# Both jobs of a step between the two layers of the first attention, with three PSUM banks for jobs and two tiles for the first layer

## The chip, the cores and the metric

The kernel runs on one core of a Trainium2 chip. The metric is the device time of one execution in microseconds. The number to be explained is the median over repeated runs.

The core has a tensor engine (PE), a vector engine (DVE), a scalar engine (ACT), a general engine (POOL) and a DMA issuing engine (SP). Each takes its instructions in the order in which the program lists them. PE writes its products to PSUM[...]. A bank holds one tile of 128 x 512 floats. DVE or ACT must read a bank out before PE may write it again.

## The reference

The program is one decoder layer on `x` of 16 x 256 x 256: a first attention, a cross attention with a context, and a routed feed-forward of four experts. Each is followed by `x = layernorm(x + part(x))`. The change touches the first attention alone:

```python
Q, K, V = x @ wq + bq, x @ wk + bk, x @ wv + bv     # 16 heads of 16 values
def prep(t):                                         # the two layers
    h1 = tanh(einsum('bshd,do->bsho', t, w1) + b1)   # 16 -> 256
    return einsum('bsho,on->bshn', h1, w2) + b2      # 256 -> 16
qp, kp = prep(Q), prep(K)
# a fixed 8x8 mixing and a rotation among the first 8 batches, then
qq, kk = sum(qe ** 2, -1), sum(ke ** 2, -1)
s = qq[:, :, None, :] * kk[:, None, :, :]
out = einsum('bijh,bjhd->bihd', softmax(s / s, axis=2), V) @ wo + bo
```

## The kernel before

The 16 batches are taken in eight pairs (`q`, `NPAIR = 8`), with 512 tokens each. `TileContext` has the orders of PE, ACT and DVE set by hand (`manual_schedule`): each engine gets its instructions in the order in which the Python code issues them.

**The steps.** The first attention runs in steps `t` from 0 to 128 (`LAST`), 16 to a pair: 8 for keys (`side` 0) and 8 for queries (`side` 1). In each, `hidden(t)` makes half of the first layer's 256 outputs for four of the 16 heads: four products `ph<-qT,w1p` with a contraction of 32 rows, into two tiles of two banks each, and two tanh on ACT (L873, `h<-ph`, 128 x 1024). `outer(t - 1, ...)` makes the second layer of the step before: four products `pe<-h,w2p` of 32 columns each, gathered over four steps in one bank (pool `psAe`). After the fourth, DVE (`enc`, L890) or ACT (`sq`, L893) reads that bank out.

**The plan.** Everything else is listed in `Plan`. There are two kinds of entry:

- Entries with a fixed step (`plan.at`), which `plan.run(t)` issues: `scores` (DVE, L967, `z<-rqb,ra`), `exps` (ACT, L974, `z<-z`), `spread` (a DMA on SP's queue, `rqb<-rqd`) and `norm` (DVE and POOL).
- Jobs with a first and a last step (`plan.job`). `plan.take()` issues the one whose last step comes first. A job is a group of products or transposes on PE into one bank and the read-out of that bank by DVE (in a few cases ACT): `turn_x` (`ptx`), `project` (`pq`), `values` (`pv`), `rotate` (`pr`), `norms` (`p`), `queries` (`ptr`), `weigh` (`po`, the values weighed by `z`), `finish1` to `finish3` (`pn`, `pto`, `pf`). The generators that `fold` advances are jobs too: `pt`, `pp`, `pb` of the feed-forward's weights and `pex` of the cross attention's.

**A step's order**, in `step` (L1145 on): `hidden(t)`, one job, the fixed entries of `t`, `outer(t - 1)`, a second job. On PE this reads: `ph`, job, `pe`, job.

**PSUM** while the first attention runs:

```python
ps = heads.enter_context(tc.tile_pool(name="psA", bufs=1, space=PSUM))    # jobs
pse = heads.enter_context(tc.tile_pool(name="psAe", bufs=1, space=PSUM))  # second layer
psb = heads.enter_context(tc.tile_pool(name="psAb", bufs=3, space=PSUM))  # first layer, two banks each
```

This is 1 + 1 + 6 = 8 banks. All jobs share the single bank of `psA`. The first layer has three tiles and a step takes two, so the tiles of step `t + 1` are one that was free and the one that the first tanh of step `t` reads.

After step 128 these pools close. The cross attention's steps begin, and the last jobs of pair 7 are taken among them with the same `step` function.

## Time and profile before

| What | Value |
|---|---|
| Median of 3 runs | 1849.65 us (1845.53 to 1854.64) |
| The profiled execution, its own time | 1787.34 us |
| Its span, first to last instruction | 1785.6 us |
| Granted PE clock, mean over the span | 0.965 |
| PE / DVE / ACT / POOL busy over the span | 93% / 53% / 54% / 30% |
| First `ph` of step 0 | 11.87 us |
| First `ph` of step 9 | 45.22 us |
| First `ph` of step 127 | 560.09 us |
| `ph` products, `pe` products | 1024 records each (two for one product) |
| tanh (L873) | 256, 1112 ns each |

The profiled execution is 62 us shorter than the median of the runs. All durations here are of that execution.

A timeline row gives the start, the time until the last end, the engine, the line, the operation, the output and inputs by name, the shapes and the count. In brackets is the idle time of the engine before the row and what ended it. A step is read on PE from one `ph` row to the next. Ends of PE's products are modelled and lie about 0.1 us after the point where the next group may start, so the cost of a group is best read from start to start. A weight load (PEld) overlaps a product.

### The profile page before, as it was taken

Reading aid. Unit: us, or ns where it says so; the run is one execution under the profiler, and the core shown is the slowest. Engines: PE = TensorE matmul, PEld = TensorE weight load, DVE = VectorE, ACT = ScalarE, POOL = GpSimd, SP = SyncE. Lnnn points to the kernel's source line nnn. Section 1 sums busy time; section 2 is a strip of 40 time slices with the busy share of each in tenths; the row PEclk is TensorE's granted clock in tenths of the full one; section 3 lists DMA queues with packets and bytes.
Section 4 is the critical chain, followed back from the end, with each engine's and each line's share of the span. In section 5 each row is a group of like instructions: output and inputs, shape, how many; then the busy total and the mean of one; then the engine's idle time right before and its main releaser. Section 6 shows DMA issues by size and latency. Waiting matters only on the chain. (4 is left out here: it accounts for less than half of the span.)

```text
span 1785.6 us, 32366 instructions
## 1 busy us (share of the span) xinstructions
PE 1654.0 (93%) x12254; PEld 946.1 (53%) x12254; DVE 953.1 (53%) x2008; ACT 961.7 (54%) x1404; POOL 536.7 (30%) x1235
## 2 busy tenths in 40 slices
PE   7999999999999999999999999998999997899960
PEld 2343434343444566566565656655665666566640
DVE  2235556655555877877778676772113533122147
ACT  4556777776777766766666676654332112232242
POOL 5100313212123232445535464455321011121042
PEclk8999999999999999999999999998999999899985
DMA  9921211122212300001000000002241102321033
GB/s 262 295 81 61 68 61 61 62 70 78 65 61 72 107 14 2 15 3 38 26 15 29 11 26 9 32 26 80 75 147 50 48 13 66 109 66 42 29 98 112
DMA packets 117771, 115.34 MB, mean 65 GB/s; under 512 B 7776, under 2 KB 111408, under 8 KB 117584
## 3 DMA queue, kind: packets, MB, share of 16 engines
q1 hardware_dynamic: 108560, 93.08, 16.4%
q0 software_dynamic: 7824, 19.65, 3.7%
q8 instruction: 114, 1.87, 0.4%
q14 instruction: 73, 0.60, 0.1%
q10 hardware_dynamic: 1200, 0.15, 0.1%
HBM read 73.79 MB, written 38.54 MB: 63 GB/s over the span
## 5 line engine op out<-in xcount | busy, mean ns | idle before, releaser
L1329 DVE TENSOR_REDUCE mpad<-p 128x4 f32<-128x1024 f32 x256 | 310.6, 1216 | 107.2 <-PE p L119 104.7
L873 ACT ACTIVATE h<-ph,L_attn_b 128x1024 f32<-128x1024 f32 x256 | 271.3, 1112 | 158.5 <-PE ph L119 154.8
L1335 ACT ACTIVATE e<-p 128x512 f32<-128x512 f32 x512 | 276.4, 596 | 147.7 <-PE p L119 145.4
L119 PE MATMUL p<-qp,kT 32*128 32x256 f32 x2048 | 307.3, 402 | 1.4 <-ACT e L1335 0.6
L119 PE MATMUL p<-kT,qp 32*128 32x256 f32 x2048 | 292.6, 400 | 3.5 <-DVE mpad L1329 3.5
L119 PEld LDWEIGHTS p<-kT,qp 32*128 32x128 f32 x2048 | 183.4, 184 | 89.6 <-issue 45.2
L119 PEld LDWEIGHTS p<-qp,kT 32*128 32x128 f32 x2048 | 204.0, 185 | 7.1 <-issue 3.1
L119 PE MATMUL ph<-qT,w1p 32*128 32x512 f32 x1024 | 151.3, 648 | 3.0 <-ACT h L873 1.8
L967 DVE TENSOR_TENSOR z<-rqb,ra 128x1024 f32<-128x1024 f32 x120 | 151.5, 1265 | 3.8 <-DMA rqb<-rqd 3.5
L119 PE MATMUL pe<-h,w2p 128*32 128x512 f32 x1024 | 139.6, 617 | 1.9 <-ACT sq L893 1.0
L974 ACT ACTIVATE z<-z 128x1024 f32<-128x1024 f32 x120 | 127.1, 1060 | 1.3 <-DVE z L967 0.9
L119 PE MATMUL pob<-e,vaug 128*32 128x512 f32 x1024 | 125.9, 610 | 0.0
L632 POOL DMA_INDIRECT ya<-xlist,place x52 | 49.7, 956 | 199.9 <-DVE xs L642 68.9
L159 POOL TENSOR_SCALAR ln_ve<-ln_mv 128x2 f32<-128x2 f32 x32 | 7.2, 224 | 299.0 <-DVE ln_mv L157 298.8
L480 ACT ACT_TABLE_LOAD x18 | 23.1, 1283 | 114.1 <-PE pt L479 113.8
L119 PE MATMUL pw<-xeT,L_ffn_sw_w 128*128 128x512 f32 (+1 forms) x256 | 83.3, 486 | 1.3 <-ACT xeT L480 1.3
L163 POOL TENSOR_SCALAR xs<-xs,ln_mv,rs_y 128x256 f32<-128x256 f32 x64 | 83.2, 1305 | 3.5
L119 PE MATMUL po<-z,vaug 128*32 128x256 f32 x1024 | 72.8, 389 | 6.4 <-DVE ra L927 1.6
L119 PE MATMUL pr<-L_ffn_ml_w,hid 128*128 128x256 f32 x288 | 65.1, 388 | 8.5 <-ACT hid L547 8.5
L1384 POOL TENSOR_TENSOR ob<-o,o 128x256 f32<-128x256 f32 x32 | 23.2, 724 | 163.3 <-DVE o L1382 163.3
L119 PEld LDWEIGHTS ph<-qT,w1p 32*128 32x128 f32 x1024 | 42.7, 185 | 53.8 <-issue 42.0
L405 POOL DMA_INDIRECT xlist<-xs,place x64 | 62.8, 981 | 20.0 <-issue 17.3
(355 smaller groups left out, 2616.2 us busy)
## 6 DMA issues: line engine op xcount, KB each, us to landing
rqb<-rqd SPq DMA_DIRECT2D x64, 512.0 KB
xlist<-zero SPq DMA_DIRECT2D x16, 1024.0 KB
xe<-xlist SPq DMA_DIRECT2D x20, 512.0 KB
xlist<-ye SPq DMA_DIRECT2D x14, 512.0 KB
xs<-in_x SPq DMA_DIRECT2D x8, 512.0 KB
cx<-in_ctx SPq DMA_DIRECT2D x8, 512.0 KB
qp<-st SPq DMA_DIRECT2D x256, 2.0 KB
out<-xs SPq DMA_DIRECT2D x8, 512.0 KB
```

The costliest lines, as they stand in the source:

```text
L119: PE.matmul(out=out_, lhsT=lhsT, rhs=rhs, start=start, stop=stop)
L159: POOL.tensor_scalar(ve, mv[:, :, 1], EPS, None, ALU.add)
L163: POOL.tensor_scalar(x, x, mv[:, i, 0:1], r[:, i:i + 1], ALU.subtract, ALU.mult)
L405: put = POOL.indirect_dma_start(xlist[g][:], bass.IndirectOffsetOnAxis(ap=place[:, n, k:k + 1], axis=0), xs[:, q * CPB + n, :], None)
L480: copies[c](t[:, c, :n * P], pt[:, :n * P])
L632: POOL.indirect_dma_start(t[:, n, :], None, xlist[group(q)][:], bass.IndirectOffsetOnAxis(ap=moe["place"][:, q * CPB + n, k:k + 1], axis=0),)
L873: ACT.activation(h, phs[gp], AF.Tanh, bias=b1[:, fc:fc + 1])
L967: DVE.tensor_tensor(z, bc(rqbs[u][:, 2 * gp:2 * gp + 2], 2, 2), bc(rk, 3, S), ALU.mult)
L974: ACT.activation(z, z, AF.Exp)
L1329: DVE.tensor_reduce(mpads[j % 2][:, 2 * gp:2 * gp + 2, :, ic], p1, AX.X, ALU.max, negate=True)
L1335: ACT.activation(e[:, gi], p2[gi], AF.Exp)
L1384: POOL.tensor_tensor(o[:, ic], oas[0], oas[1], ALU.subtract)
```

## The change

`take` can now issue several jobs and keep those of one name (`behind`) to the end. `step` runs the fixed entries of `t` first, then takes both jobs, `weigh` behind the other, and only then issues `outer(t - 1)`. On PE a step reads `ph`, job, job, `pe`. The pools of PSUM become 3 banks for jobs, 1 for the second layer, and two tiles (4 banks) for the first layer: 8 again.

```diff
-    def take(self, slack=10**6):
+    def take(self, slack=10**6, n=1, behind=None):
 
-        if self.jobs:
-            best = min(self.jobs, key=lambda x: x[:2])
-            if best[0] <= self.now + slack:
+        held = []
+        for _ in range(n):
+            best = min(self.jobs, key=lambda x: x[:2], default=None)
+            if best is not None and best[0] <= self.now + slack:
                 self.jobs.remove(best)
-                best[2](*best[3])
+                if best[2].__name__ == behind:
+                    held.append(best)
+                else:
+                    best[2](*best[3])
+        for x in held:
+            x[2](*x[3])
...
-    ps = heads.enter_context(tc.tile_pool(name="psA", bufs=1, space=PSUM))
+    ps = heads.enter_context(tc.tile_pool(name="psA", bufs=3, space=PSUM))
     pse = heads.enter_context(tc.tile_pool(name="psAe", bufs=1, space=PSUM))
-    psb = heads.enter_context(tc.tile_pool(name="psAb", bufs=3, space=PSUM))
+    psb = heads.enter_context(tc.tile_pool(name="psAb", bufs=2, space=PSUM))
...
             if t < LAST:
                 hs = hidden(t)
-            plan.take()
             plan.run(t)
+            plan.take(n=2, behind="weigh")
             if last[0] is not None:
                 outer(t - 1, last[0])
             last[0] = hs
-            plan.take()
```

The cross attention's own plan calls `take` with its defaults, which do what they did.

## The prediction, made before the changed kernel was run

> **What bounds the kernel now.** I read the busy times by stage, then what PE waited for, then PE's timeline step by step. The stretch from step 9's first `ph` to step 127's holds the first attention at full load:

> ```profile
> core 0: us, PE busy (x) PEld busy (x) DVE busy (x) ACT busy (x) POOL busy (x), PEclk, DMA share, GB/s
> ...
> 45.22:560.09 514.87, 500.65 (x3652) 208.60 (x3648) 271.81 (x434) 357.42 (x362) 104.75 (x226) 0.99 0.28 87
> ```

> PE is busy 97%, ACT 69%, DVE 53%: PE sets the pace, 4.36 us a step (514.87 / 118). So only what shortens PE's own sequence or its waits can help. Those waits, in the same stretch:

> ```profile
> engine line waited for: us in total, times, longest us
> PE pex L1197 <- DVE scr L1195: 4.8, 3, 2.9
> PE po L119 <- DVE ra L927: 1.6, 2, 0.9
> PE ptx L838 <- PE ph L119: 1.5, 2, 0.7
> PE po L119 <- DVE xT L839: 1.4, 1, 1.4
> ...
> PE pb L119 <- PE pb L119: 0.5, 1, 0.5
> PE pb L119 <- DVE rowsof L269: 0.5, 1, 0.5
> ```

> With the rows left out the list sums to 14.1 us. `po` waiting for `ra` or `xT` is no matter of data: these read out the previous job's bank. The timeline shows one such step:

> ```profile
> 334.09 1.14 PE L119 MATMUL ph<-qT,w1p 32*128 32x512 f32 x8
> ...
> 335.16 1.98 PE L119 MATMUL pq<-xT,L_attn_wq 128*128 128x512 f32 x4
> 335.34 2.12 ACT L873 ACTIVATE h<-ph,L_attn_b 128x1024 f32<-128x1024 f32 x2 [2.48 <-PE ph L119]
> ...
> 337.07 1.07 PE L119 MATMUL pe<-h,w2p 128*32 128x512 f32 x8
> ...
> 338.07 0.66 PE L838 MATMUL ptx<-ident,xs 128*128 128x128 f32 x4
> ...
> 338.65 1.14 PE L119 MATMUL ph<-qT,w1p 32*128 32x512 f32 x8
> ...
> 340.45 0.66 DVE L839 COPY xT<-ptx 128x512 f32<-128x512 f32 x1
> ...
> 341.16 1.07 PE L119 MATMUL po<-z,vaug 128*32 128x256 f32 x16 [1.37 <-DVE xT L839]
> ```

> From start to start, `ph` takes 1.07, `pq` 1.91, `pe` 1.00, `ptx` 0.58. At 341.16 `po` has waited for DVE, which came late to `xT`. The ACT row gives the second figure I need: tanh begins 1.25 us after its `ph` and both take 2.12.

> [...] In the experts' stage groups of one mode follow without loss:

> ```profile
> 1329.13 1.04 PE L479 MATMUL pt<-ident,xe 128*128 128x128 f32 x8
> 1330.01 3.62 PE L119 MATMUL pw<-xeT,mw 128*128 128x256 f32 x16
> 1333.53 3.72 PE L119 MATMUL pr<-L_ffn_me_c2w,hid 128*128 128x256 f32 x16
> ```

> Eight transposes take 0.88, 0.11 each, so four are 0.43; between groups of other modes four took 0.58. `pq` takes 1.91 where its four records, 0.43 apart, make 1.71. A drain costs 0.15 to 0.20. [...] after the 2.9 us wait for `scr` at 415.6, PE ran at 0.50 from 417.2 to 420.6, and `pe` took 1.88. The 1.37 us wait above did not do it. [...] So with one bank, a job's products wait for the last read-out.

> **The change, part by part** (PE groups counted from both programs' instruction orders, steps 9 to 126).

> *Fewer drains.* A step's two jobs were each between two other modes. Now they adjoin, and in 48 steps both use the whole array. The order shows 404 changes of mode before and 357 after. 47 x 0.16 = **-7.5 us**. `weigh` behind the other job changes nothing here: `po` and `pe` share a mode (0.88 instead of 1.00) and adjoined before too.

> *Three banks for jobs.* Of the 14.1 us, 1.0 are the feed-forward's `pb`, a chain of data that stays. The rest waits behind a read-out or a late DVE. With three banks a group waits only for the job three before. To 13.1 I add 1.5 for the half clock after 415.6 (`po` 0.6, `pe` 0.9) and 1.5 for some fifteen waits that modelled ends shorten by 0.1: 16 us at stake. `pex` still needs `scr` of DVE in its own step; I take **-15** (-10 to -16).

> *Two tiles for the first layer.* Now `ph` of the next step waits for both tanh. The least distance of two `ph` is 1.25 + 2.12 + 0.11 (tanh end to product, from 30.50 to 30.61 below) = 3.48 us. With three tiles it was one tanh less:

> ```profile
> 29.44 2.12 ACT L873 ACTIVATE h<-ph,L_attn_b 128x1024 f32<-128x1024 f32 x2
> ...
> 30.61 1.24 PE L119 MATMUL ph<-qT,w1p 32*128 32x512 f32 x6 [1.77 <-ACT h L873]
> ...
> 42.00 2.12 ACT L873 ACTIVATE h<-ph,L_attn_b 128x1024 f32<-128x1024 f32 x2 [0.28 <-PE ph L119]
> ...
> 44.40 2.12 ACT L873 ACTIVATE h<-ph,L_attn_b 128x1024 f32<-128x1024 f32 x2 [0.28 <-PE ph L119]
> ```

> In the last two rows tanh pairs stand 2.40 apart. The new order has 28 steps shorter than 3.48: two without a job (2.07 long, 1.41 short each), seven with `po` alone (2.95, 0.53), seven with one or two small transposes (about 2.65, 0.83), twelve with two small groups (about 3.15, 0.33). 2.8 + 3.7 + 5.8 + 4.0 = **+16.3**. A longer step hides the wait, since `ph` starts later anyway; the average is 4.1. The lightest step keeps PE at work for half of 3.48 us; I expect no half clock.

> *Steps 0 to 8* have few jobs. Steps 6 to 8 took 2.07, 2.41 and 2.40; at 3.48 they cost +3.6. Steps 2 and 3 lose as much, but step 4 waits for ACT's sine tables (26.6 to 29.4) anyway. The first `pq` no longer waits for a bank, -1. Sum **+2.5** (0 to +5).

> *The end.* After step 127 jobs wait for the bank by 0.55, 0.55 and 0.89, and a half clock follows. That is 3.5 us; further on PE waits for `exps` of the last pair, so I take half, **-2**.

> *Moved at no cost.* The fixed entries now stand ahead of both jobs. On DVE, a score (1.22) precedes the first read-out; two banks more cover it, and with one bank it would cost PE up to 1.2 us a step. On ACT `exps` (1.05) precedes `rotate`'s square, needed a step later. On SP, `spread`'s DMA goes ahead of `queries`' store in the same step; no pair's spread needs a store of its own step. On POOL, `norm` goes ahead of `turn_x`'s add; POOL is busy 20%. `pe` moves behind both jobs: the tanh it reads ended a step before, and its bank is read out under the next `ph` (1.07) and jobs. DMAs keep their number and size. The later parts keep their order.

> **Sum**: -7.5 - 15 + 16.3 + 2.5 - 2 = -5.7, say -6 us. That is 1781 against the profiled 1787.3, and 1849.65 - 6 = **1843.5** against the median, which lies 62 us above the profiled execution. Its own range is -13 to +1. A measurement here can tell some 0.5%, 9.2 us, from no change, so the forecast lies inside that bound and its range crosses it.

> **The rivals.**

> *The tile wait is mostly hidden.* The runs take 3.5% longer than the profiled execution. If that is PE, steps lengthen, while tanh does not: at 4% the 16 us fall to about 14. If the early steps also cost nothing, all 16 us of waits go and the end keeps its 3.5, the change gives -7.7 - 16 + 14 - 3.5 = -13, and with drains at 0.20 -15: **1834.5**. For it: PE is the bound nearly everywhere. Against: the short steps are in the order, and the wait needs nothing unusual.

> *The tanh chain becomes the bound, slower.* Between two tanh pairs, ACT has 1.36 us for `exps` (1.05) and every fourth step a square (0.69). If a score comes late from DVE, which now reads out both jobs in a row, `exps` pushes the next tanh and the distance of two `ph` grows. At 3.7 the short steps sum to 27 us, at 3.9 to 38, at 4.0 to 44. The gains less the early loss are 22, so it decides from 3.6 on; 0.5% slower is reached at 3.8. At 3.9: -22 + 38 = +16, **1865.5**. For it: 56 of 118 steps lie under 3.7. Against: a score is issued a whole step before its `exps`, and DVE is half idle.

> *It does not do what it says*: the waits for banks turn into waits for the same late DVE in the next step, +15, cancelling the gain: 1849 to 1858. The trace speaks against it: late read-outs there are single events.

> **How the numbers follow.** Forecast 0.60, of which 0.22 lies beyond 9.2 us. First rival 0.23, faster. Second 0.14, slower. Third 0.03, of which 0.01 slower. Faster 0.45, same 0.40, slower 0.15. The likeliest case stays 1843.5, its own range 1836.5 to 1850.5. The range over the cases runs from 1830, below the first rival, to 1860, well into the second.

> **What would show it.** Right: PE's waits for DVE read-outs nearly gone; a new row `ph` waiting for ACT's `h` of about 16 us in some 28 times plus 5 early; `ph` never closer than 3.45; step 9 begins near 47.7 and step 127 near 554. Wrong: `ph` waiting for `h` by over 25 us, or waits of `pex`, `po` and `pn` for DVE still over 8 us.

## The result and the profile after

The changed kernel took **1858.71 us** (median of 19 runs, 1849.93 to 1866.73). The kernel before took 1845.94 us beside it (19 runs, 1836.91 to 1855.7). The ratio is 1.006, 95% interval 1.0042 to 1.0079: **0.6% slower**. Repeated beside the kernel before, it came to 1.0068 (1.0047 to 1.0089) on a second chip and 1.005 (1.0033 to 1.0067) on a third. The forecast was 1843.5, a gain of 6 us, so the sign was wrong.

One thing is needed to read the numbers below. On some chips the kernel before takes some 1784 us, on others some 1847, so times are compared only within one chip. The changed kernel differs as much between chips (1791.7 and 1858.7 us), and 63 of those 67 us lie in its cross attention (668 us in e14, 731 in the first profile).

I read the stage first. Its line for the changed kernel, from step 9's first `ph` to step 127's:

```profile
core 0: us, PE busy (x) PEld busy (x) DVE busy (x) ACT busy (x) POOL busy (x), PEclk, DMA share, GB/s
48.07:574.44 526.37, 514.42 (x3664) 221.50 (x3661) 277.02 (x441) 358.16 (x361) 102.77 (x239) 0.98 0.27 83
```

The stage takes 526.4 us where it took 514.9. It ends at 574, not near 554. In three profiles of the changed kernel, on chips of both kinds, it took 524.1 to 526.4; in four of the kernel before 513.2 to 515.1. PE is still 98% busy in it, and its mean clock fell from 0.99 to 0.98. What PE's products waited for there:

```profile
engine line waited for: us in total, times, longest us
PE pex L1202 <- DVE scr L1200: 9.1, 7, 2.8
...
PE ph L125 <- ACT h L879: 0.6, 2, 0.3
```

All waits for read-outs of the bank have gone, as forecast. `pex` waits for `scr` twice as long as before (9.1 against 4.8). The wait for a tile hides from this list: `ph` waits for `h` by 0.6 us only, because PE's wait shows on the weight load ahead of the product (75 such waits in the stage, 57.1 us of weight load idle, most of it under other products). The steps must be read from start to start. This is the step that surprised me, in the timeline of the changed kernel:

```profile
509.23 1.14 PE L125 MATMUL ph<-qT,w1p 32*128 32x512 f32 x8
...
512.16 1.63 PE L125 MATMUL ph<-qT,w1p 32*128 32x512 f32 x8
...
512.65 0.31 PEld L125 LDWEIGHTS ph<-qT,w1p 32*128 32x128 f32 x6 [0.20 <-ACT h L879]
513.44 0.69 ACT L899 ACTIVATE sq<-pe,b2c 128x512 f32<-128x512 f32 x1
513.72 2.27 PE L125 MATMUL p<-selc,sq 128*128 128x16 f32 x16
...
515.83 3.58 PE L125 MATMUL pq<-xT,L_attn_wk 128*128 128x512 f32 x4
...
519.35 1.06 PE L125 MATMUL pe<-h,w2p 128*32 128x512 f32 x8
```

The step before had `po` alone, so this `ph` is stretched by the tile wait to 1.56 from start to start, 0.49 more than 1.07. Then comes `p`, the norms' product, 16 columns wide, held up a little by its square `sq` on ACT (2.11 from start to start, 1.89 in e15 below). Then `pq` takes 3.52 instead of 1.91: the granted clock was 0.50 from 515.70 to 519.11. In the old order `pe` stood between `ph` and `p` (in e15, this `p` runs from 506.07 to 507.96, and the `ph` behind it takes its full-clock 1.07).

For the whole span the best pair is the changed kernel and the kernel before on one chip (e14 and e15 below, spans 1789.0 and 1780.9). Stage lines of the changed kernel, with the same columns as above: steps 0 to 8, steps 9 to 126, cross attention up to its last `pob`.

```profile
0.00:48.45 48.45, 37.97 (x170) 12.67 (x170) 13.16 (x48) 22.42 (x22) 25.60 (x53) 0.89 0.92 258
48.45:574.30 525.85, 513.96 (x3668) 221.16 (x3664) 276.91 (x441) 358.08 (x361) 102.57 (x239) 0.98 0.27 84
574.30:1242.20 667.90, 658.30 (x6670) 401.21 (x6670) 482.09 (x901) 430.94 (x801) 297.66 (x778) 0.99 0.08 26
```

The kernel before beside it:

```profile
0.00:44.70 44.70, 33.03 (x167) 11.89 (x167) 12.74 (x47) 21.85 (x21) 24.92 (x52) 0.92 0.91 258
44.70:559.80 515.10, 500.63 (x3652) 208.30 (x3648) 271.72 (x434) 357.47 (x362) 104.76 (x226) 0.99 0.28 87
559.80:1234.00 674.20, 664.61 (x6683) 405.22 (x6686) 485.33 (x908) 431.37 (x802) 297.96 (x790) 0.99 0.08 26
```

The changed kernel loses 3.75 us in steps 0 to 8 and 10.75 after them, and gets 6.3 back in the cross attention: +8.2, with the spans 8.1 apart. Some of this is only moved. PE has 16 more records before step 127: one `pv` and one `pf` of four products each (two records a product) are done earlier, 1.92 + 1.92 = 3.8 us of work. So the stage really loses 6.9, and the cross attention really gains 2.5.

I split the stage by group of products, from start to start. Each group has a base time when nothing waits, read from the kernel before (`ph` 1.07, `pq` 1.91, and so on). What exceeds it goes to the wait ahead of the next product, or to the half clock where the clock record shows one. Both columns sum to the stage. Another choice of base times moves its rows by up to about 1 us.

| Steps 9 to 126, us (e14 and e15) | before | changed |
|---|---|---|
| Products without waits | 494.0 | 487.6 (of it 3.8 moved from later) |
| Waits of the job after `ph` and others, mostly for banks | 10.1 | 2.8 |
| `ph` waiting for a tile | none | 13.5, in 24 steps |
| `pex` waiting for `scr` | 5.05 | 9.6 |
| `pb`'s own chain | 2.75 | 2.6 |
| Lost to half clock | 3.3 | 9.8 |
| Sum | 515.1 | 525.8 |

### The profile page after: what moved, and what is told of

Same layout as the page of the kernel before. It is cut to its first block, busy times and chain, and to the rows that moved or that the text cites. A ratio compares the mean times of both kernels' runs of the same rounds, so it can differ in the third digit from the quotient of the medians.

```text
span 1857.0 us, 32348 instructions
## 1 busy us (share of the span) xinstructions
PE 1703.1 (92%) x12254; PEld 975.3 (53%) x12254; DVE 955.5 (51%) x2008; ACT 965.8 (52%) x1404; POOL 534.6 (29%) x1235
## 5 line engine op out<-in xcount | busy, mean ns | idle before, releaser
L125 PE MATMUL p<-qp,kT 32*128 32x256 f32 x2048 | 325.9, 414 | 26.5 <-ACT e L1340 13.5
L125 PE MATMUL p<-kT,qp 32*128 32x256 f32 x2048 | 308.6, 411 | 3.5 <-DVE mpad L1334 3.3
L125 PEld LDWEIGHTS p<-kT,qp 32*128 32x128 f32 x2048 | 189.3, 189 | 92.3 <-issue 47.7
L125 PEld LDWEIGHTS p<-qp,kT 32*128 32x128 f32 x2048 | 211.8, 191 | 40.2 <-issue 19.0
L125 PE MATMUL ph<-qT,w1p 32*128 32x512 f32 x1024 | 166.4, 653 | 4.4 <-ACT h L879 3.3
L125 PEld LDWEIGHTS ph<-qT,w1p 32*128 32x128 f32 x1024 | 49.0, 186 | 123.2 <-ACT h L879 68.8
L1366 ACT COPY ovTb<-pob 128x512 f32<-128x512 f32 x64 | 37.6, 587 | 60.8 <-PE pob L125 56.6
```

Of the source, the lines that this page charges most:

```text
L125: PE.matmul(out=out_, lhsT=lhsT, rhs=rhs, start=start, stop=stop)
L1366: ACT.copy(o, po)
```

## The experiments

Fifteen runs follow, some of them repeats that share a chip with others (e1, e2, e4, e5; e6 to e9; e10 to e12; e13 to e16). "Stage" is step 9's first `ph` to step 127's, "half" is the half-clock loss by the split above, in us. The ratio is of medians. The other columns are of one profiled execution each, and that lies 10 to 18 us above the median for e4, e5, e7, e9 and e10 and 20 us below it for e8, so small differences between them show little.

| Run | ratio to before (95%) | stage | tile wait | `pex` | half |
|---|---|---|---|---|---|
| e15 before | 1 | 515.1 | none | 5.05 | 3.3 |
| e14 changed | 1.005 (1.0033 to 1.0067) | 525.8 | 13.5 | 9.6 | 9.8 |
| e13 order alone | 1.0655 (1.0636 to 1.0675) | 636.0 | 1.9 | 9.1 | 34.2 |
| e2 pools alone | 1.0021 (1.001 to 1.0032) | 517.1 | 11.6 | 5.2 | 4.8 |
| e4 generators first | 1.005 (1.0029 to 1.0072) | 522.8 | 13.5 | 4.7 | 11.3 |
| e5 filler | 1.0038 (1.0022 to 1.0054) | 522.4 | 6.4 | 9.6 | 6.5 |
| e10 norms behind | 1.0017 (0.999 to 1.0043) | 520.0 | 13.4 | 9.6 | 6.5 |
| e7 five tiles | 1.0036 (1.0017 to 1.0055) | 525.3 | 6.1 | 9.8 | 12.9 |
| e8 five tiles, generators first | 1.0022 (0.9998 to 1.0046) | 516.0 | 6.3 | 4.5 | 8.1 |
| e9 five tiles, old order | 1.0012 (0.9991 to 1.0033) | 512.9 | 7.6 | 5.4 | 3.2 |
| e11 all three repairs | 0.9959 (0.9938 to 0.9981) | 511.1 | 6.1 | 4.8 | 8.0 |
| e16 the same, other chip | 0.9958 (0.9941 to 0.9974) | 512.5 | 6.1 | 4.5 | 9.5 |

The column "tile wait" holds whatever delays the group after `ph`; in e13 and in the five-tile kernels not all of it is for a tile.

### The changed kernel and the kernel before on one chip: e14, e15

> The changed kernel once more, beside e15 (the kernel before) on the same chip. Theory: ratio 1.006 to 1.009; step 9's ph at 48 to 49, step 127's at 573 to 575, 10 to 12 us later than e15's; the cross attention (from step 127's first ph to the last pob) within 5 us of e15's, 670 to 685 on a chip that runs the kernel before in some 1784 us, 728 to 745 on one that takes some 1847. Rival (the change itself lengthens the cross attention): it is 30 us or more longer than e15's.

> The kernel before, for the same chip's profile. Theory: step 127's ph at 558 to 560; the cross attention as long as e14's within 5 us. Rival: 673 us whatever the chip.

Measured: 1791.73 us, ratio 1.005 (1.0033 to 1.0067), just below the theory's figure; e15 1782.62. Step 9's `ph` at 48.5, step 127's at 574.3, 14.5 us later than e15's, more than the 10 to 12 that I named. The cross attention is 6.3 us shorter, of which 3.8 is the work moved ahead. The rival falls: the change doesn't lengthen the cross attention.

Three more runs bear on the chips. The kernel before, run again:

> The kernel before, unchanged, profiled once more. Its first profile showed 1787 us where its runs have a median of 1846, so the two profiles can't be compared after the first attention. First theory (the loss lies in the first attention: tile wait, half clock, late pex): this profile shows about 1846, step 127's first ph near 560 us as in the first profile, and the missing 60 us as half-clock windows in the cross attention, like those that the changed kernel's profile has there. Rival (the loss lies in the cross attention): step 127 at 560, but from there to the end at least 10 us less than the changed kernel's 1282 us.

It took 1779.92 us, not some 1846, with a stage of 513.2 and a cross attention of 673.8; its chip runs the kernel before in 1783. It was the first sign that the 62 us between my profile and the median belong to the chip.

> The changed kernel, unchanged, as the measure for the runs beside it: the earlier runs were on a chip whose kernel before takes 1783 us, not 1846. First theory (its loss lies in the first attention, 10 us up to step 127's first ph, and nowhere else): 1.005 to 1.007 of before, as on the other chip. Rival (the cross attention takes part of it, with a clock that differs from chip to chip): a ratio of 1.000 to 1.003 here.

Measured: 1860.37 us against 1847.28, ratio 1.0068 (1.0047 to 1.0089), stage 524.1, cross attention 728.1.

> The kernel before, profiled beside these runs. If the chip is the one of 1846 us: first theory (the changed kernel loses only up to step 127, the cross attention is the same and differs by chip): 728 to 740 us from step 127's first ph to the last pob, like the changed kernel's 728 and 731. Rival (the cross attention loses too): under 722. On the other chip it tells nothing new: 673.

Measured: 1783.67 us, stage 514.8, cross attention 674.0. It fell on a chip of the faster kind, so alone it told nothing new.

### The pools alone: e2

Against the kernel before:

```diff
-    ps = ... tc.tile_pool(name="psA", bufs=1, space=PSUM)
+    ps = ... tc.tile_pool(name="psA", bufs=3, space=PSUM)
-    psb = ... tc.tile_pool(name="psAb", bufs=3, space=PSUM)
+    psb = ... tc.tile_pool(name="psAb", bufs=2, space=PSUM)
```

> The kernel before with the new pools alone (3 job banks, two first-layer tiles), its order of a step kept (ph, job, pe, job). First theory (two tiles cost the wait for both tanh, 25 steps of this order are shorter than 3.48 us and sum to 15 us, +2.5 in steps 0 to 8; three banks give back 10 to 15): between 1844 and 1856, with ph waiting for h for about 15 us. Rival (it is the order, two read-outs behind each other on DVE, that costs): 10 us faster than before, 1836.

Measured: ratio 1.0021 (1.001 to 1.0032), stage 517.1, step 9's `ph` at 47.4. The banks' waits of 10 us are gone and a tile wait of 11.6 has come, so these two nearly cancel. What remains, against e1 on the same chip, is 2.8 us in steps 0 to 8 and 3.2 us of half clock (4.8 against 1.6).

### The order alone: e13

Against the changed kernel, as are the edits further on unless the text says otherwise:

```diff
-    ps = ... tc.tile_pool(name="psA", bufs=3, space=PSUM)
+    ps = ... tc.tile_pool(name="psA", bufs=1, space=PSUM)
-    psb = ... tc.tile_pool(name="psAb", bufs=2, space=PSUM)
+    psb = ... tc.tile_pool(name="psAb", bufs=3, space=PSUM)
```

> The order of the change (fixed entries, both jobs, then pe) with the pools of the kernel before (one bank for jobs, three tiles of two banks for the first layer). Theory (half clock and pex's waits, not the order as such, ate the gain; and the order needs the banks): the 47 fewer mode changes still give -6 us, the tile wait of some 15 us is gone, but the second job now stands right behind the first job's read-out in the one bank. The read-out is 0.66 us of DVE, with 0.2 us on either side, and behind a score of 1.22 us in half of the steps: 0.9 to 1.5 us for each of some 90 steps with two jobs, +80 to +130 us, so step 127's ph some 600 to 640, and a ratio of 1.04 to 1.07. Rival (the waits in the single bank are mostly hidden, since pe and ph stand between, and the loss of the change comes from its two tiles alone): step 127 near 545 to 560, ratio 0.99 to 1.00.

Measured: 1902.12 us, ratio 1.0655 (1.0636 to 1.0675), step 127's `ph` at 681.4. The ratio is as expected, but step 127 begins 41 us past the theory's upper end. From start to start there are 95 waits of 1.0 us on average, as expected; the 34 us lost to half clock were not in my sum. Rows of the timeline of e13:

```profile
357.79 1.94 PE L125 MATMUL pr<-enc,mix 128*64 128x512 f32 x12
...
360.92 0.59 ACT L919 ACTIVATE sq<-pr 128x512 f32<-128x512 f32 x1
361.57 0.30 PEld L125 LDWEIGHTS pq<-xT,L_attn_wk 128*128 128x128 f32 x2 [2.29 <-ACT sq L919]
```

`pr` and `pq` share the bank. With `pe` no longer between two jobs, `pq` waits until ACT has read `pr` out behind tanh and `exps`. So the order needs the banks; the two parts are not separate gains.

### `pex` first, so that its read-out has a step's room: e4

```diff
-                if best[2].__name__ == behind:
+                if behind and best[2].__name__ != "fold":
                     held.append(best)
                 else:
                     best[2](*best[3])
+        held.sort(key=lambda x: x[2].__name__ == behind)
```

> The changed kernel, but a fold (the generators of the weights, pex among them) goes ahead of the step's other job. First theory (pex as a second job waits for scr, which stands on DVE behind the first job's read-out: 1.41 us three times, 1.3 once): 5 us faster than the changed kernel, 1853.5, and the row pex waiting for scr falls by 5 us. Rival (these waits are the DMA of the raw weights or lie under the tile wait): no change, 1858.7.

Measured: ratio 1.005 (1.0029 to 1.0072), stage 522.8. The waits of `pex` fall from 9.6 to 4.7, about the figure of the kernel before, so the cause of the added 4.9 is shown. In the changed kernel `pex` came second, and DVE was behind. Timeline of e14:

```profile
432.53 0.75 DVE L855 TENSOR_SCALAR qT<-pq,L_attn_bk 128x512 f32<-128x512 f32 x1 [2.25 <-PE pq L125]
...
433.20 0.28 DVE L1200 TENSOR_TENSOR scr<-rawwk2T,mask8b 128x128 f32<-128x128 f32 x1
433.63 0.30 PE L1202 MATMUL pex<-ident,scr 128*128 128x128 f32 x1 [1.13 <-DVE scr L1200]
```

`scr` needs nothing of `pq`, but it is issued after `pq`'s read-out `qT`. DVE sat idle for 2.25 us until `pq`'s products were done, ran `qT` at 432.53 and only then `scr`, at 433.20. The stage is 3.0 us shorter than e14's: half clock took back 1.5 (23.9 us of it in the stage, loss 11.3; near 108, behind `pb`'s one-column products, it lasted 10.2 us where the changed kernel has 3.4). The whole time shows no gain, but 3 us would lie within the intervals of e4 and e14.

### Small products that fill the short steps: e5

`names` lists the step's jobs and `LONG` how long each kind takes (the lines that fill them are left out):

```diff
...
             if last[0] is not None:
                 outer(t - 1, last[0])
+                spare = 3.48 - 2.07 - sum(LONG.get(n, 0.5) for n in names)
+                if 1 < t < LAST and spare > 0.2:
+                    n = min(512, int(spare / 0.43 * 256) // 32 * 32)
+                    idle = banks[0].tile([P, 512], F32, tag="sm", name="idle")
+                    mm(idle[:32, :n], w2p[:, 0, 0, :], last[0][0][:, 0, :n])
```

> The changed kernel with one product without use behind pe in each step that has few jobs, as long as the step is short of 3.48 us, in the same mode as pe and into a job bank that nobody reads. It fills the wait for tanh with work and takes no wait away. First theory (the waits leave windows of 3.4 us with too little work, the clock halves in them and costs 1.7 us each): the half-clock windows near 406, 516 and 550 us are gone, 5 us faster than the changed kernel, 1853.5. Rival (the half clock comes from the norms' thin products, whatever stands beside them): no change, 1858.7, or up to 5 us slower where a filler is too long.

Measured: ratio 1.0038 (1.0022 to 1.0054), stage 522.4. The half-clock windows near 516 and 550 are gone (the loss falls to 6.5). Against the first profile of the changed kernel, that near 406 is gone too and one at 333 has come; e14 has these two as e5 has them. Step by step the filler takes the time that the tile wait took (tile wait 6.4, other excess 11.3 against 2.8), so it can at best give back the half clock. It supports the half clock's part without isolating it well.

### Five single tiles for the first layer: e7, e8, e9

The same eight banks, cut otherwise: two for jobs, one for the second layer, and five tiles of one bank, with four tanh of 128 x 512 instead of two of 128 x 1024.

```diff
-    ps = ... tc.tile_pool(name="psA", bufs=3, space=PSUM)
+    ps = ... tc.tile_pool(name="psA", bufs=2, space=PSUM)
-    psb = ... tc.tile_pool(name="psAb", bufs=2, space=PSUM)
+    psb = ... tc.tile_pool(name="psAb", bufs=5, space=PSUM)
...
-            phs = [psb.tile([P, 2, 512], F32, tag="big", name="ph") for _ in range(2)]
-            for g in (0, 2, 1, 3):
+            phs = [psb.tile([P, 512], F32, tag="big", name="ph") for _ in range(4)]
+            for g in range(4):
...
-                ACT.activation(h, phs[gp], AF.Tanh, bias=b1[:, fc:fc + 1])
+                for k in range(2):
+                    ACT.activation(h[:, k], phs[2 * gp + k], AF.Tanh, bias=b1[:, fc:fc + 1])
```

e7 is the changed order with this cut:

> The changed kernel with its PSUM cut otherwise: two job banks, and the first layer in five tiles of one bank with four tanh of 128 x 512 in place of two of 128 x 1024. The order stays. A product of the next step then waits for the third tanh at most, and the next step's first tanh needs one product alone. First theory (the two-tile wait costs 16 us, 2.5 in steps 0 to 8, and most of the half clocks hang on it): 18 to 25 us faster than the changed kernel, 8 to 14 faster than before, no wait of ph for h. Rival (it is the order: read-outs one behind the other on DVE): no faster than the changed kernel, since two banks are fewer than three.

Measured: ratio 1.0036 (1.0017 to 1.0055), 5.6 us faster than the changed kernel beside it (e6) and not 18 to 25. The wait after `ph` falls from 13.5 to 6.1, but there are eight half-clock windows in the stage, four of them at a `p`. PE's waits in e7:

```profile
PE pex L1203 <- DVE scr L1201: 9.3, 7, 2.9
PE p L125 <- ACT sq L900: 2.6, 6, 0.7
```

The second row is new: with `ph` no longer late, `p` is too early for its square. This made me form the next theory, that the thin `p` right behind `ph` is where the clock goes.

e8 adds the edit of e4 to e7:

> As the run before, and a fold goes ahead of the step's other job. First theory (late pex is a second, separate cost of 4 to 5 us): 4 us faster than with five banks alone, 12 to 18 faster than before. Rival (what fold first gained was only a shift of half-clock windows): no difference to five banks alone.

Measured: ratio 1.0022 (0.9998 to 1.0046), stage 516.0, `pex` 4.5, half-clock loss 8.1. It is 2.8 us faster than e7, which is within the noise, and not faster than the kernel before.

e9 has the five tiles with the old order:

> The kernel before with that cut of PSUM (two job banks, five tiles of one bank) and its own order ph, job, pe, job. It tells what the order is worth when the first layer doesn't wait. First theory (the order saves 7.5 us of drains and costs 5 by late pex): 0 to 4 us slower than five banks in the new order, 6 to 12 faster than before. Rival (the order is what costs): at least 5 us faster than five banks in the new order.

Measured: ratio 1.0012 (0.9991 to 1.0033), stage 512.9. It is 4 us faster than e7 and level with e8, so the new order had gained nothing yet, against the theory. The stage is 2 us better than that of the kernel before, yet the time is not. Its cross attention took 745 us on this slower chip, with the old order of jobs, so a long cross attention doesn't come with the new order.

### The norms behind the other job: e10

```diff
-                if best[2].__name__ == behind:
+                if behind and best[2].__name__ in ("norms", behind):
                     held.append(best)
                 else:
                     best[2](*best[3])
-        for x in held:
+        for x in sorted(held, key=lambda x: x[2].__name__ == behind):
             x[2](*x[3])
```

> The changed kernel, but norms (the thin products p of 16 columns) goes behind the step's other job, ahead of weigh alone: ph, pq, p, pe in place of ph, p, pq, pe. Five banks took most of the tile wait away and the half-clock windows stayed, so the first theory now reads: the half clock comes where p follows ph directly[...]; the old order had p between pe and ph with no wait. Expected: no window of half clock at the p of steps 89, 113 and 121, 4 to 6 us less up to step 127's first ph than the changed kernel's 524, ratio to before 1.003 to 1.005. Rival (the waits for tanh alone make the windows): the same windows, no gain, 1.007.

Measured: ratio 1.0017 (0.999 to 1.0043), stage 520.0, half-clock loss 6.5. The interval overlaps that of e14, so in the whole time a gain is not resolved; the stage is 4 to 6 us shorter than in the changed kernel's profiles. The same step as above, in e10's timeline:

```profile
511.78 1.63 PE L125 MATMUL ph<-qT,w1p 32*128 32x512 f32 x8
513.33 1.99 PE L125 MATMUL pq<-xT,L_attn_wk 128*128 128x512 f32 x4
515.15 1.85 PE L125 MATMUL p<-selc,sq 128*128 128x16 f32 x16
516.94 1.06 PE L125 MATMUL pe<-h,w2p 128*32 128x512 f32 x8
```

The tile wait is the same (1.55 to the next start), but `pq` takes 1.82 and the clock stays at 1.00: the windows near 516 and 550, which all three profiles of the changed kernel have, are gone, and no others came. Now see how little PE did in the window ahead of a half clock. Two pieces of 3.41 us of e14, the one before the half clock and the half clock itself (columns as in the stage lines):

```profile
512.54:515.95 3.41, 3.35 (x25) 2.42 (x24) 0.46 (x2) 3.41 (x5) 1.50 (x1) 1.00 0.14 49
515.95:519.36 3.41, 3.41 (x8) 0.88 (x11) 0.80 (x3) 1.08 (x2) 0.00 (x0) 0.50 0.00 0
```

PE counts as 98% busy (3.35 of 3.41 us), and the granted clock of the next piece is 0.50 all the same. By an estimate from the records, a 512-column record of `pq` takes 0.43, so the 16 thin records of `p` stream for 16 x 0.43 / 32 = 0.2 us. With some 0.75 of `ph` and 0.2 of `pq`, PE streams columns for about 1.2 of 3.41 us, a share of 0.35. In e10 the two windows around the same step reach 0.64 and 0.58 by the same estimate, and both have a clock of 1.00.

The clock record of the changed kernel's first profile has six half-clock pieces in the stage. They last 3.41 us each and start whole multiples of 3.413 us apart (106.1, 191.4, 406.5, 423.5, 515.7, 549.8). In the 3.41 us ahead of them PE was busy for 3.41, 2.90, 3.35, 0.92, 3.35 and 3.35 us, so its busy share does not show which window comes before a half clock.

How much PE streamed ahead of a half clock can be estimated from the traces. Each profile's clock record gives a grid of 3.413 us. For every window of the stage that ran at full clock, in all 17 profiles, take the share of time in which PE streams columns by the estimate above: 0.43 us for 512 columns, from `pq`'s records. Products whose records overlap count once (the eight 512-column records of a `ph` take 1.07 us together, the four of a `pq` 1.91).

| Estimated share of the window | windows | followed by half clock |
|---|---|---|
| under 0.36 | 63 | 63 |
| 0.36 to 0.39 | 22 | 15 |
| over 0.39 | 2410 | 0 |

This is a count over the windows of this stage, and its line moves with the estimate: with each record's columns spread over the record's whole length, the first profiles of the two kernels have 295 such windows; the 8 at 0.19 to 0.34 were followed by half clock and the 287 from 0.38 on were not. PE's busy share draws no such line: of the 2170 windows with PE busy 97% or more, 18 were followed by half clock. Waits and thin products count alike in the estimate. It also fits that half clock moves between like kernels: the chain of `pex` that fills 0.386 of its window in e14 (PE busy 1.81 of 3.41 us, then 0.50 from 331.6) lies 0.1 us earlier on the grid in the first profile of the changed kernel, fills 0.421 (1.92 of 3.41), and the next piece has a clock of 1.00. And the old order was not free of it: in e15 half clock at 402.1 follows a `p` that stands behind `pe`, in a window with an estimated share of 0.39.

### All three repairs together: e11, e16

Five tiles, generators first, norms behind the other job: the diffs of e7 and e4, with this order.

```diff
+        held.sort(key=lambda x: (x[2].__name__ == behind) * 2 + (x[2].__name__ == "norms"))
```

> Five banks and fold first, and norms behind the other job: the changed order with its three costs taken out. First theory (tile wait, late pex and half clock are the whole loss): 505 to 512 us from step 9 to step 127's first ph, though 3.8 us of jobs more lie in it than in the kernel before, where it is 513 to 515; ratio to before 0.996 to 1.000. Rival (something else in the order costs): at least 516 us, ratio over 1.002.

> The kernel of e11 (five one-bank tiles for the first layer, two job banks, generators first, norms behind the other job) on the chip of e14 and e15. Theory: step 127's ph at 557 to 560, ratio 0.994 to 0.998 on either chip. Rival (its gain hung on the faster chip): ratio 1.000 to 1.004.

Measured: 1776.78 us, ratio **0.9959 (0.9938 to 0.9981)**, and 1776.65 us, ratio 0.9958 (0.9941 to 0.9974), the latter beside e14. It beats the kernel before by 0.4% and the changed kernel by 15 us on one chip. The stage is 511.1 and 512.5, with the 3.8 us of work moved ahead in it. So the three repairs together undo the loss; how much each is worth alone in the whole time was not resolved. In e16 half clock still costs 9.5, around 103 to 117 behind `pb`'s one-column products, and at 195 and 332 where `pb` and `pex` keep PE waiting. Both ran on chips of the faster kind, so what it gives on the others was not measured.

## Why the prediction was wrong, point by point

The comparison is e14 against e15, one chip, one profile each.

- **What bounds the stage: right.** PE's own sequence sets the pace before and after.
- **Fewer drains, -7.5, with 1.5 for short waits that modelled ends hide: right.** Products without waits fell by 6.4 with 3.8 us of work more, so -10.2 where the two terms make -9.0. No run takes the drains alone, but the groups show them: where two jobs of one mode adjoin in e14 and nothing waits, the first is 0.09 shorter and the second 0.02 to 0.10 (`pq` ahead of `pv`: 1.82 and 1.82, instead of 1.91 and 1.92). A "drain" is no more than this measured difference; what PE does at a change of mode was not shown.
- **Two tiles, +16.3: right in kind, a little large.** It is 13.5 in 24 steps. The least distance was set at 3.48, but tanh pairs stand 3.41 apart, and 28 x 0.07 = 2.0. Rows of the changed kernel's first steps, where 2.40 stood before:

```profile
39.84 2.12 ACT L879 ACTIVATE h<-ph,L_attn_b 128x1024 f32<-128x1024 f32 x2 [1.87 <-PE ph L125]
43.25 2.12 ACT L879 ACTIVATE h<-ph,L_attn_b 128x1024 f32<-128x1024 f32 x2 [1.29 <-PE ph L125]
```

- **The landmarks of that step: half wrong.** "`ph` never closer than 3.45" fails, since the first product (two of the eight records) starts as soon as one tile is free: 509.23 and 512.16 above are 2.93 apart, and the other six records wait inside the group. And the row of 16 us cannot be read from PE's waits, where it shows as 0.6.
- **Three banks, -15: the first step that failed, at `pex`.** Without the 1.5 of small waits and the 1.5 of half clock in it, -12 was meant. Bank waits gave -10.1. But `pex` went up by 4.55 instead of down, and other waits, such as `p` for its square, took 2.8. With `pb`'s -0.2 that makes -2.95. The prediction wrote that "`pex` still needs `scr` of DVE in its own step" and then let most of that wait go. It did not ask what stands ahead of `scr` on DVE once `pex` is the second job; e4 shows that it is the first job's read-out.
- **"I expect no half clock": the step that failed outright.** The sum had -1.5 for it; it was +6.5, a miss of 8.0. I had checked the lightest step only, "PE at work for half of 3.48 us", as if busy time and an idle wait were what decide. That was my own estimate, and no trace had shown it. The profile of before had shown otherwise (rows below): PE busy for 2.90 of 3.40 us, much of it with `pb`'s one-column products, and then half clock. The windows near 516 and 550 come with the 16-column `p` right behind a stretched `ph`, which the drains' saving had put there; e10 removes them by order alone. In one sense the same move gave and took: dropping `pe` from between two jobs saves a drain and takes away the dense work around the thin one (by the estimate above a share of 0.35 ahead of the half clock in e14, 0.64 and 0.58 in e10). Those near 106, 192, 332 and 424 stand at the chains of `pb` and `pex`.

```profile
181.70:185.10 3.40, 2.90 (x24) 2.45 (x27) 0.42 (x3) 3.00 (x3) 0.03 (x1) 1.00 0.45 140
185.10:188.50 3.40, 3.40 (x16) 1.23 (x12) 3.40 (x8) 0.00 (x0) 3.40 (x6) 0.50 0.32 85
```

- **Steps 0 to 8, +2.5: right in kind**, 3.75 here and 2.85 between the first profiles. **The end, -2: right**, -6.3 with 3.8 of it moved work.

In sum, predicted -7.5 - 15 + 16.3 + 2.5 - 2 = -5.7. Measured, in the same order and with the half clock by itself: -10.2 - 2.95 + 13.5 + 3.75 - 2.5 + 6.5 = +8.1. Of the 13.8 between them, 9.0 are `pex` and the other waits, 8.0 the half clock, 1.25 the first steps; the better drains, tiles and end give back 4.5.

Of the rivals, the hidden tile wait did not occur: the early steps cost 3.75 and the waits of `pex` grew. The slower one named ACT, with tanh pushed apart by `exps` to 3.9; pairs stand at 3.41, so it was slower by another mechanism. "It does not do what it says" was nearer: bank waits turned into a wait for the same DVE, but only for `pex`. That its upper figure of 1858 is the time measured is chance, since it stood for another sum.

What stays open is why some chips run the cross attention in some 730 to 745 us and others in some 670. The profiles narrow it down: in the cross attention of the first profile of the changed kernel PE has no product running eight times, for 1.6 to 3.8 us, 23.4 us in all and mostly some 86 us apart, and 91 us pass at half clock. In e14 there is one such gap, of 1.5, and 14 us of half clock. By an estimate, gaps and half clock (at half its length) make 61 of the 63 us between them. What makes the gaps was not found. The half clock also repeats least well of all parts: it cost 8.2 to 9.9 in three profiles of the changed kernel, 1.6 to 3.3 in four of the kernel before.

## What to carry to other kernels

When two groups of products are moved together to save drains, ask of every stretch of 3.4 us that remains how many columns PE streams in it, not how busy it looks (in this stage, by the estimate above, half clock followed all windows with a share under 0.36 and none over 0.39), and try thin products beside dense ones (in e10 the windows near 516 and 550 were gone). When a job that needs another engine first is moved to second place, look at what the first job puts ahead of it on that engine. And with the number of PSUM banks kept, cut the tiles before moving banks between pools: tiles of one bank with half-size tanh took away over half of the tile wait that two tiles of two banks made (13.5 to 6.1 us, e7).
